# Block ends and routes of a graph convolution placed between node tiles of the next block, with what its scatters read kept for the program

## The chip, the cores and the metric

The kernel runs on one core of a Trainium2 chip, in one launch. The metric is the device time in microseconds (us) of one execution. A run of several executions gives a median; one execution is also recorded by the hardware profiler, and its span (first to last instruction) is what the views of the profile show. In these views PE is the matrix engine (TensorE), PEld its weight loads, DVE is VectorE, ACT is ScalarE, POOL is GpSimd and SP is SyncE. "L1431" is line 1431 of the kernel's source.

## The reference

The input is a matrix `x` of 3125 nodes by 256 features and 50,000 edges (`src`, `dst`). Four blocks follow each other, each on a normalised copy of `x` and each added to it:

```python
x = x + gcn(layernorm(x))       # three graph convolutions
x = x + ffn0(layernorm(x))      # 16 experts, 2 of them for each node
x = x + gat(layernorm(x))       # attention over the edges, 4 heads of 64
x = x + ffn1(layernorm(x))      # 8 experts, 2 of them for each node

# one graph convolution, three times (the third without relu)
h   = (h * norm_src[:, None]) @ W
agg = segment_sum(h[src], dst)
h   = relu(agg * norm_dst[:, None] + b)

# ffn0; ffn1 is of the same kind, with gelu
logits = x @ gate_w + gate_b
vals, idx = top_k(logits, 2);  w = softmax(vals)
y = x + sum_k w[k] * (relu(x @ w1[idx[k]] + b1[idx[k]]) @ w2[idx[k]] + b2[idx[k]])
y = layernorm(y) * gamma + beta
```

## The kernel before

**Nodes and stages.** The 3125 nodes lie in 25 node tiles (`NT`) of 125 real rows in 128 partitions. `X` holds the features, `HB` a normalised copy. The stages of the profiled execution are, in us of the span: the edges are counted into a dense matrix of counts in DRAM, `cnt`, and its transpose `cntT` (to about 308); the three convolutions (308 to 476, 476 to 641, 641 to 857); the plan of the first experts and the first experts (to about 1235); the attention, GAT (to about 1770); the second experts (to the end).

**A convolution.** The columns of `cnt` (destination nodes) are cut into seven blocks, `BLK`: four of 512 and three of 384 columns. At the start of a layer every node tile of `HB` is split into two parts, a rounded one and the rest, in `parts` (DVE L1417 and its neighbour, ACT L1419). Then, for each block, the 25 node tiles are taken in five groups of five. For a group the counts are loaded (`cload`, five DMAs a block on SP's queue) and cast on ACT to `ar` (L1426; two buffers). For each node tile four matrix products add to the two PSUM tiles `agg` (L1431), so a block has 100 of them. At the block's end `agg` is copied to `aT`, half by DVE (L1434) and half by ACT (L1435). For each of the block's three or four node tiles, PE multiplies `aT` by the layer's weights into `gout` (L1440), DVE scales it and adds the bias (`gy`, L1443), and ACT writes relu of it to `HB` (L1446); in the third layer (layer 2) DVE adds it to `X` (L1448) instead.

**A route.** After a block of layer 2, its rows are normalised again and routed: `moments` (DVE L692, L693, L695; the square root on ACT, L675; `newton` on DVE, L680 to L685), `normalise` (DVE, L703), and `R0.route`, which runs the generator `Router.steps` to its end. These steps are, in order:
- PE transposes the rows (L805) and ACT copies them to `hb` (L807), tile by tile; PE computes the gate's logits (L812).
- DVE finds the two best experts of each node (`lg`, L821, to L851). The rows are sent to DRAM (`keep`, POOL's queue, L785).
- A small tile `meta` of 8 values per node is filled: the node's number (L858), the second expert (L859), the two weights (the exponential on ACT, L866; L868 to L870), zeros (L871) and the number as an integer (L872). The combining weights `cw` follow (L876 to L878).
- `both` and `seen` count the nodes of each expert (L882 to L885), and two products on PE, L889 and L890, give `pr`, the place of each node within its expert. From it DVE computes `at`, with `off` for the padding rows (L899), and the places `at_i` (L903).
- POOL scatters one row block of `meta` after the other into `slots` in DRAM by these places (L905), eight for a block of four tiles. The scatters are declared independent of each other.

`meta`, `off` and `at_i` are taken from a pool with two buffers for each name, so a third route writes to the buffers of the first one.

After the last block `R0.plan` counts the tiles of each expert (L923 to L957). `experts` then reads the slots (`slot`, DMAs on ACT's queue, L1015), gathers rows (`xs`, POOL, L1017), transposes them (L1026), multiplies by the first weights (L1038; `w1t` loaded at L1003) and the second (L1048). At its beginning the combining weights are transposed and copied to `cT` (ACT, L1090), for the product with the second biases (L1099).

**The attention** runs over the same seven blocks on `cntT`. Its work at a block's end is already a generator, `finish`, of which one step is taken after each node tile of the next block; for every second block, and after the last, the last steps include `R1.steps`, the route of the second experts. All products on PE stand in one chain:

```python
if last:
    tc.add_manual_dep(m.ins, last[0].ins.name, ...)   # no semaphore: an order only
last[:] = [m]
```

**What sets the order.** Each engine executes its own list of instructions in order. A scheduler at build time makes these lists from the dependencies, the buffers' reuse and the order of the program's text, so an instruction can stand on its engine before or after others than the text shows. In the convolutions of the kernel before, no order is written out; in the attention the chain fixes PE's.

Of the kernel before, what the change touches and what calls it, by code (L numbers as in the profile page):

```python
# [19 lines left out]
P = 128  # L20
# [574 lines left out]
def fast(  # L595
# [68 lines left out]
    ns = consts.tile([P, NT], F32, name="ns")  # L664
# [70 lines left out]
    tok_i = consts.tile([P, NT], I32, name="tok_i")  # L735
    nc.gpsimd.iota(tok_i, pattern=[[P, NT]], base=0, channel_multiplier=1)

    class Router:


# [2 lines left out]
        def __init__(self, name, gate_w, gate_b, E, softmax, pool):  # L743
            self.name, self.E, self.softmax = name, E, softmax
            self.Q = E * NT + 3
            self.TT = -(-2 * N // P) + E
            self.slots = dram.tile([self.Q * P, 8], F32, name=f"slots_{name}")
            self.feats = dram.tile([NP, D], F32, name=f"feats_{name}")
            self.res = dram.tile([2 * NP + self.TT * P, D], F32, name=f"res_{name}")
            self.sent = []  # L750
            self.gwt = pool.tile([P, DC, E], F32, name=f"gw_{name}")
            nc.sync.dma_start(self.gwt, gate_w.rearrange("(c p) e -> p c e", p=P))
            self.gbt = row_bcast(gate_b, E, f"gb_{name}", pool)
            self.cw = pool.tile([P, NT, E], F32, name=f"cw_{name}")
# [32 lines left out]
        def steps(self, H, t0, U, work, psum, h0=None, pe=lambda i: i, kept=None):  # L787
# [4 lines left out]
            def wt(name, shape, dt=F32):  # L792
                return work.tile(shape, dt, name=f"{name}_{nm}", tag=f"{name}_{nm}")
# [58 lines left out]
                                                   op0=OP.mult, op1=OP.add)  # L852
                    cur = rest
            yield
            meta = wt("meta", [P, U, 8])
            if not kept:
                self.keep(H[:, h0:h0 + U, :], t0, U)
            nc.vector.tensor_copy(meta[:, :, 0], tok2[:, t0:t0 + U])  # L858
            nc.vector.tensor_scalar(meta[:, :, 1], firsts[1], float(E), None, op0=OP.add)  # L859
            if self.softmax:  # L860
                nc.vector.tensor_copy(meta[:, :, 2], tops[0])
# [1 line left out]
            else:  # L863
# [4 lines left out]
                nc.vector.tensor_scalar(p1, ex, 1.0, None, op0=OP.add)  # L868
                nc.vector.reciprocal(meta[:, :, 2], p1)
                nc.vector.tensor_mul(meta[:, :, 3], ex, meta[:, :, 2])  # L870
            nc.vector.memset(meta[:, :, 4:], 0.0)  # L871
            nc.vector.tensor_copy(meta.bitcast(I32)[:, :, 5], tok_i[:, t0:t0 + U])  # L872
            yield
            cw = self.cw[:, t0:t0 + U, :]
            w2 = wt("w2", [P, U, E])
            nc.vector.tensor_tensor(cw, hots[0], bc(meta[:, :, 2]), op=OP.mult)  # L876
            nc.vector.tensor_tensor(w2, hots[1], bc(meta[:, :, 3]), op=OP.mult)
            nc.vector.tensor_tensor(cw, cw, w2, op=OP.add)  # L878
            yield

            both = wt("both", [P, U, E], BF16)
# [12 lines left out]
            for i in range(2):  # L894
                at = wt(f"at{i}", [P, U])
                nc.vector.tensor_tensor(hots[i], hots[i], row, op=OP.mult)
                nc.vector.tensor_reduce(at, hots[i], axis=AX.X, op=OP.add)
                off = wt(f"off{i}", [P, U])
                nc.vector.tensor_scalar(off, drop[:, t0:t0 + U], float((E * NT + 1) * P + i * PADS), unreal,  # L899
                                        op0=OP.add, op1=OP.mult)  # L900
                nc.vector.scalar_tensor_tensor(at, at, real, off, op0=OP.mult, op1=OP.add)
                at_i = wt(f"at_i{i}", [P, U], I32)
                nc.vector.tensor_copy(at_i, at)  # L903
                for u in range(U):
                    d = nc.gpsimd.indirect_dma_start(  # L905
                        out=self.slots, out_offset=bass.IndirectOffsetOnAxis(ap=at_i[:, u:u + 1], axis=0),
                        in_=meta[:, u, :], in_offset=None)
# [492 lines left out]
    with tc.tile_pool(name="gcn", bufs=2) as gp, \  # L1400
            tc.tile_pool(name="gparts", bufs=1) as gh, \
            tc.tile_pool(name="gloads", bufs=3) as loads, \
            tc.tile_pool(name="ps_agg", bufs=2, space=PSUM) as ps_agg, \
            tc.tile_pool(name="ps_gout", bufs=2, space=PSUM) as ps_gout, \
            tc.tile_pool(name="ps_gmisc", bufs=2, space=PSUM) as ps_gmisc:
        def misc(shape):
            return ps_gmisc.tile(shape, F32, name="misc", tag="misc")

        R0.ready(f0_b1, f0_b2, plans)
        parts = gh.tile([P, NT, 2, D], F32R, name="parts")  # L1410
        for layer in range(3):
            for t in range(NT):
                if layer == 0:
                    nc.vector.tensor_scalar(HBn[:, t, :], X[:, t, :], mv[:, t, 0:1], rn[:, t:t + 1],
                                            op0=OP.subtract, op1=OP.mult)
                hi = gp.tile([P, D], F32, name="hi", bufs=3)
                nc.vector.tensor_single_scalar(hi.bitcast(I32), HBn[:, t, :D].bitcast(I32), -4096,  # L1417
                                               op=OP.bitwise_and)
                nc.scalar.copy(parts[:, t, 0, :], hi)  # L1419
                nc.vector.tensor_tensor(parts[:, t, 1, :], HBn[:, t, :D], hi, op=OP.subtract)  # L1420
            for b, (s0, w) in enumerate(BLK):
                agg = [ps_agg.tile([P, 512], F32, name=f"agg{f}") for f in range(DC)]
                for kg in range(0, NT, KG):
                    a = load_cnt(loads, cnt[b], kg, w)
                    ar = gp.tile([P, KG, 512], F32R, name="ar")
                    nc.scalar.copy(ar[:, :, :w], a[:, :, :w])  # L1426
                    for k in range(KG):
                        t = kg + k
                        for f in range(DC):
                            for i in range(2):  # L1430
                                nc.tensor.matmul(agg[f][:, :w], parts[:, t, i, f * P:(f + 1) * P], ar[:, k, :w],  # L1431
                                                 start=(t == 0 and i == 0), stop=(t == NT - 1 and i == 1))
                aT = gp.tile([P, DC, 512], F32, name="aT")
                nc.vector.tensor_copy(aT[:, 0, :w], agg[0][:, :w])  # L1434
                nc.scalar.copy(aT[:, 1, :w], agg[1][:, :w])  # L1435
                for u in range(w // P):
                    t = s0 // P + u
                    po = ps_gout.tile([P, D], F32, name="gout")
                    for f in range(DC):
                        nc.tensor.matmul(po, aT[:, f, u * P:(u + 1) * P], gw[layer][:, f, :],  # L1440
                                         start=(f == 0), stop=(f == DC - 1))
                    y = gp.tile([P, D], F32, name="gy", bufs=3)
                    nc.vector.scalar_tensor_tensor(y, po, nd[:, t:t + 1], gb[layer],  # L1443
                                                   op0=OP.mult, op1=OP.add)
                    if layer < 2:
                        nc.scalar.activation(HBn[:, t, :D], y, AF.Relu, scale=ns[:, t:t + 1])  # L1446
                    else:
                        nc.vector.tensor_add(X[:, t, :], X[:, t, :], y)  # L1448
                if layer == 2:
                    mv, r = moments(X, s0 // P, w // P)  # L1450
                    normalise(HBn, X, mv, r, s0 // P, w // P)
                    R0.route(HBn, s0 // P, w // P, gp, misc)
        R0.plan(plans, misc)

    gconst.__exit__(None, None, None)
# [26 lines left out]
    with tc.tile_pool(name="moe0", bufs=1) as mp:  # L1482
# [16 lines left out]
        with tc.tile_pool(name="ps_pre", bufs=2, space=PSUM) as ps, tc.tile_pool(name="tail", bufs=1) as mp:  # L1499
# [274 lines left out]
```

## Time and profile before

| what | value |
|---|---|
| median of 3 runs | 2113.64 us (2106.36 to 2114.82) |
| profiled execution's own time | 2094.98 us |
| its span | 2093.2 us, so 1.8 us lie around it |
| mean granted clock of PE | 0.956 |
| PE / DVE / ACT / POOL busy | 90% / 57% / 38% / 18% |
| sums of the convolutions, PE L1431 | 447.8 us in 2100 products |
| block-end products, PE L1440 | 78.3 us in 300, 20.5 us idle ahead of them |
| scatters of the routes, POOL L905 | 107.8 us in 100 |
| casts of the counts, ACT L1426 | 220.8 us in 105 |

Busy time is the sum of an engine's instructions; the idle time beside a group is what the engine stood still just before it, with the instruction or transfer whose end released it. In a timeline a row starts with the start in us and the time that the row covers, then engine, line, operation, tiles written and read, shapes and the number of instructions taken together; a bracket at the end is the idle time before it. In a chain of waits, the three numbers are us in total, number of waits and the longest. In the table of stretches the columns are the stretch, its length, then for PE, PEld, DVE, ACT and POOL the busy time with the number of instructions, then PE's granted clock (1.00 is full speed), the DMA share and GB/s. The profiled execution is 18.7 us shorter than the median of the runs.

### The profile page before, as it was taken

The page shows a single profiled execution, that of the slowest core. Times are in us where ns is not written, and L with a number is a line of the kernel's source. Part 1 is how long each engine was busy: PE and PEld are TensorE (multiplying, and loading weights), DVE is VectorE, ACT ScalarE, POOL GpSimd, SP SyncE. Part 2 cuts the span into 40 slices and gives each one's busy share as a digit, 9 for nine tenths or more (in the row PEclk, how much of TensorE's full clock was granted, in tenths as well). Part 3 has the DMA queues.
Part 4 walks back from the last instruction along what each step waited for, and adds up shares of the span by engine and source line. Part 5 has one row for each costly group of instructions (what it writes and reads, how often), then busy time and mean ns, then how long its engine had stood idle before and what let it go on. Part 6 is the DMA issues. An engine that isn't in the chain of part 4 may idle for free. (4 is left out here: it accounts for less than half of the span.)

```text
span 2093.2 us, 31963 instructions
## 1 busy us (share of the span) xinstructions
PE 1893.4 (90%) x10944; PEld 1252.0 (60%) x10944; DVE 1188.1 (57%) x3825; ACT 791.7 (38%) x1611; POOL 369.1 (18%) x414
## 2 busy tenths in 40 slices
PE   1898979999999898699998988999999998699997
PEld 1444548898898677588887741222223232588886
DVE  7998863131124344443332768899998998434330
ACT  0367766565555534222222561212212222222221
POOL 4000000000000312254443000000300402344430
PEclk9999989999999999789999989999999999599998
DMA  5145664344344333665664601111011110465656
GB/s 148 53 176 217 227 220 133 110 129 129 116 115 147 112 91 94 198 201 168 182 192 139 213 1 51 39 48 61 28 54 43 43 39 28 122 182 164 193 160 197
DMA packets 172299, 259.91 MB, mean 124 GB/s; under 512 B 33476, under 2 KB 116658, under 8 KB 171100
## 3 DMA queue, kind: packets, MB, share of 16 engines
q1 hardware_dynamic: 148446, 211.87, 32.6%
q0 software_dynamic: 16016, 37.00, 5.6%
q10 hardware_dynamic: 7662, 8.84, 1.3%
q8 instruction: 93, 1.52, 0.3%
q14 instruction: 82, 0.67, 0.1%
HBM read 187.38 MB, written 70.27 MB: 123 GB/s over the span
## 5 line engine op out<-in xcount | busy, mean ns | idle before, releaser
L1431 PE MATMUL agg<-ar,parts 128*128 128x512 f32 (+1 forms) x2100 | 447.8, 371 | 7.6 <-ACT parts L1419 7.6
L1431 PEld LDWEIGHTS agg<-ar,parts 128*128 128x128 f32 x2100 | 383.6, 189 | 55.0 <-ACT parts L1419 7.7
L1702 DVE SCALAR_TENSOR_TENSOR HB<-ub,wj,cload 128x512 f32<-128x512 f32 (+1 forms) x420 | 268.6, 689 | 21.2 <-ACT ub L1606 9.9
L1426 ACT CAST ar<-cload 128x2560 fp32r<-128x2560 f16 (+1 forms) x105 | 220.8, 2103 | 147.1 <-PE agg L1431 133.5
L1038 PE MATMUL ph<-xsT,w1t 128*128 128x128 f32 x1792 | 239.2, 285 | 12.2 <-DVE xsT L1028 11.1
L1042 ACT ACTIVATE hid<-ph,b1s 128x128 f32<-128x128 f32 x448 | 128.1, 369 | 322.0 <-PE ph L1038 310.1
L1038 PEld LDWEIGHTS ph<-xsT,w1t 128*128 128x128 f32 x1792 | 220.4, 196 | 47.0 <-DVE xsT L1028 30.5
L1048 PE MATMUL py<-w2all,hid 128*128 x896 | 211.9, 380 | 0.0
L1590 PE MATMUL att<-HB,xp 128*64 128x512 f32 (+1 forms) x840 | 187.5, 567 | 0.0
L1048 PEld LDWEIGHTS py<-w2all,hid 128*128 128x128 f32 x896 | 162.1, 191 | 17.5
L1326 DVE TENSOR_SCALAR od<-ramp,by 128x450 f16<-128x450 f16 (+11 forms) x588 | 152.3, 320 | 22.1 <-PE pc L1328 21.0
L1434 DVE COPY aT<-agg 128x512 f32<-128x512 f32 (+1 forms) x21 | 13.3, 633 | 248.5 <-PE agg L1431 248.5
L1328 PE MATMUL pc<-od,os 128*128 128x450 f16 (+11 forms) x588 | 136.6, 334 | 17.6 <-DVE od L1326 9.5
L1059 DVE TENSOR_TENSOR to_i<-to,two 128x1 int32<-128x1 f32 x112 | 17.7, 158 | 237.4 <-DMA res_m<-y,to_i 237.4
L1065 POOL DMA_INDIRECT res_m<-y,to_i x112 | 110.4, 986 | 232.6 <-DVE y L1064 228.3
L905 POOL DMA_INDIRECT slots_m<-meta_m,at_i_m x100 | 107.8, 1078 | 209.0 <-DVE at_i_m L903 122.2
L1331 ACT CAST cr<-pc 128x400 f16<-128x400 f32 (+10 forms) x202 | 95.5, 503 | 63.8 <-PE pc L1328 48.9
L1017 POOL DMA_INDIRECT xs<-feats_m,slot x112 | 108.3, 967 | 61.7 <-issue 23.8
L1590 PEld LDWEIGHTS att<-HB,xp 128*64 128x64 f32 x840 | 51.8, 137 | 107.7 <-issue 61.1
L1328 PEld LDWEIGHTS <-os 128*128 128x128 f16 x588 | 62.2, 118 | 77.9 <-DVE od L1326 20.6
L1590 PE MATMUL sums<-HB,pj 128*32 128x512 f32 (+1 forms) x840 | 102.6, 561 | 0.0
L1440 PE MATMUL gout<-g0w,aT 128*128 128x256 f32 x300 | 78.3, 417 | 20.5 <-DVE aT L1434 15.7
(332 smaller groups left out, 2350.0 us busy)
## 6 DMA issues: line engine op xcount, KB each, us to landing
cload<-cnt SPq DMA_DIRECT2D x60, 640.0 KB
w1t<-in_L_ffn_w_dram SPq DMA_DIRECT2D x56, 512.0 KB
w1t<-in_L_ffn_W_dram SPq DMA_DIRECT2D x52, 512.0 KB
cload<-cnt SPq DMA_DIRECT2D x45, 480.0 KB
cntT<-ct SPq DMA_DIRECT2D x100, 128.0 KB
cnt<-cr SPq DMA_DIRECT2D x4, 3200.0 KB
cload<-cntT SPq DMA_DIRECT2D x20, 640.0 KB
r<-res_m SPq DMA_DIRECT2D x50, 256.0 KB
```

Source lines behind the costliest of these rows:

```text
L905: d = nc.gpsimd.indirect_dma_start(out=self.slots, out_offset=bass.IndirectOffsetOnAxis(ap=at_i[:, u:u + 1], axis=0), in_=meta[:, u, :], i ...
L1017: nc.gpsimd.indirect_dma_start(out=xs, out_offset=None, in_=self.feats, in_offset=bass.IndirectOffsetOnAxis(ap=slot[:, 5:6].bitcast(I32), ...
L1038: behind(nc.tensor.matmul(ph[:, c, :], w1t[:, f, c * P:(c + 1) * P], xsT[:, f, :], start=(f == 0), stop=(f == DC - 1)), "PE")
L1042: nc.scalar.activation(hid[:, c, :], ph[:, c, :], func, bias=self.b1s[:, c, j:j + 1])
L1048: behind(nc.tensor.matmul(py, hid[:, c, :], w2all[:, bass.ds(r, 1), c, :].rearrange("p o d -> p (o d)"), start=(c == 0), stop=(c == FC - 1 ...
L1065: d = nc.gpsimd.indirect_dma_start(out=self.res, out_offset=bass.IndirectOffsetOnAxis(ap=to_i, axis=0), in_=y, in_offset=None)
L1326: nc.vector.tensor_scalar(od[:, :w * NT], ramp[:, :w * NT], by[1][:, j:j + 1], None, op0=OP.is_equal)
L1328: nc.tensor.matmul(pc[:, :w * NT], os_[:, :, j % OS], od[:, :w * NT], start=(k == 0), stop=(k == c - 1))
L1426: nc.scalar.copy(ar[:, :, :w], a[:, :, :w])
L1431: nc.tensor.matmul(agg[f][:, :w], parts[:, t, i, f * P:(f + 1) * P], ar[:, k, :w], start=(t == 0 and i == 0), stop=(t == NT - 1 and i == 1))
L1590: return chain(nc.tensor.matmul(*args, **kw))
L1702: nc.vector.scalar_tensor_tensor(e[:, h, :w], ub[:, h, :w], wj[:, t, h:h + 1], a[:, k, :w], op0=OP.max, op1=OP.mult)
```

## The change

Four things are changed.

1. All products of the convolutions on PE stand in one chain. The work at a block's end is a generator, `finish`, with the copies to `aT` first; then after each node tile of the next block one step is taken: the products of one node tile in a step, then (in layer 2) an empty step, `moments`, `normalise`, an empty step, and the steps of the route. In layers 0 and 1 the last node tiles (22 to 24) are split into `parts` within the last block's `finish`, and the next layer begins with the first 22. After the last block all steps are run to the end before the plan.
2. `metas` (8 values for all 25 tiles), `places` and, in each router, `off` are tiles kept for the program, filled at its start as far as they don't depend on the data. A route writes its own slice of them.
3. `Router.steps` has one more empty step ahead of `both`; the attention runs the same steps, so its count products (L889, L890) come one node tile later in PE's chain.
4. `lr`, a small tile of the attention, is taken from another pool.

```diff
+    metas = consts.tile([P, NT, 8], F32, name="metas")
+    nc.vector.memset(metas, 0.0)
+    nc.vector.tensor_copy(metas[:, :, 0], tok2)
+    nc.vector.tensor_copy(metas.bitcast(I32)[:, :, 5], tok_i)
+    places = consts.tile([P, 2, NT], I32, name="places")
...
+            self.off = pool.tile([P, 2, NT], F32, name=f"off_{name}")
+            for i in range(2):
+                nc.vector.tensor_scalar(self.off[:, i, :], drop, float((E * NT + 1) * P + i * PADS), unreal,
+                                        op0=OP.add, op1=OP.mult)
...
-            meta = wt("meta", [P, U, 8])
+            meta = metas[:, t0:t0 + U, :]
             if not kept:
                 self.keep(H[:, h0:h0 + U, :], t0, U)
-            nc.vector.tensor_copy(meta[:, :, 0], tok2[:, t0:t0 + U])
...
-            nc.vector.memset(meta[:, :, 4:], 0.0)
-            nc.vector.tensor_copy(meta.bitcast(I32)[:, :, 5], tok_i[:, t0:t0 + U])
             yield
             cw = self.cw[:, t0:t0 + U, :]
...
+            yield
             yield
 
             both = wt("both", [P, U, E], BF16)
...
-                off = wt(f"off{i}", [P, U])
-                nc.vector.tensor_scalar(off, drop[:, t0:t0 + U], float((E * NT + 1) * P + i * PADS), unreal,
-                                        op0=OP.add, op1=OP.mult)
+                off = self.off[:, i, t0:t0 + U]
                 nc.vector.scalar_tensor_tensor(at, at, real, off, op0=OP.mult, op1=OP.add)
-                at_i = wt(f"at_i{i}", [P, U], I32)
+                at_i = places[:, i, t0:t0 + U]
...
+        def finish(layer, b, agg):
+            s0, w = BLK[b]
+            aT = gp.tile([P, DC, 512], F32, name="aT")
+            nc.vector.tensor_copy(aT[:, 0, :w], agg[0][:, :w])
+            nc.scalar.copy(aT[:, 1, :w], agg[1][:, :w])
+            yield
+            for u in range(w // P):
+                t = s0 // P + u
+                po = ps_gout.tile([P, D], F32, name="gout")
+                for f in range(DC):
+                    chain(nc.tensor.matmul(po, aT[:, f, u * P:(u + 1) * P], gw[layer][:, f, :],
+                                           start=(f == 0), stop=(f == DC - 1)))
+                y = gp.tile([P, D], F32, name="gy", bufs=3)
+                nc.vector.scalar_tensor_tensor(y, po, nd[:, t:t + 1], gb[layer], op0=OP.mult, op1=OP.add)
+                if layer < 2:
+                    nc.scalar.activation(HBn[:, t, :D], y, AF.Relu, scale=ns[:, t:t + 1])
+                    if b == len(BLK) - 1:
+                        split(t)
+                else:
+                    nc.vector.tensor_add(X[:, t, :], X[:, t, :], y)
+                yield
+            if layer == 2:
+                yield
+                mv, r = moments(X, s0 // P, w // P)
+                yield
+                normalise(HBn, X, mv, r, s0 // P, w // P)
+                yield
+                yield
+                yield from R0.steps(HBn, s0 // P, w // P, gp, misc, pe=chain)
+
+        ends = []
+
+        def step():
+            while ends and next(ends[0], ends) is ends:
+                ends.pop(0)
...
-            for t in range(NT):
+            late = BLK[-1][0] // P if layer else NT
+            for t in range(late):
...
-                                nc.tensor.matmul(agg[f][:, :w], parts[:, t, i, f * P:(f + 1) * P], ar[:, k, :w],
-                                                 start=(t == 0 and i == 0), stop=(t == NT - 1 and i == 1))
+                                chain(nc.tensor.matmul(agg[f][:, :w], parts[:, t, i, f * P:(f + 1) * P], ar[:, k, :w],
+                                                       start=(t == 0 and i == 0), stop=(t == NT - 1 and i == 1)))
+                        step()
+                if layer < 2:
+                    while ends:
+                        step()
+                end = finish(layer, b, agg)
+                next(end)
+                ends.append(end)
+        while ends:
+            step()
         R0.plan(plans, misc)
...
-    lr = g1.tile([P, NT, 2, NH], F32, name="lr")
...
+            lr = mp.tile([P, NT, 2, NH], F32, name="lr")
```

`chain` is the function quoted above, now also for the convolutions; `split` holds the three operations that fill `parts`.

More of the change, by code (lines that the diff above doesn't have):

```diff
@@ L1410, in fast, with chain, split @@
         parts = gh.tile([P, NT, 2, D], F32R, name="parts")
+        last = []
+        def chain(m):
+            if last:
+                tc.add_manual_dep(m.ins, last[0].ins.name, mybir.DependencyInfo(
+                    mybir.DependencyClass.NoSync, mybir.DependencyReason.DATA), reason="in this order")
+            last[:] = [m]
+            return m
+        def split(t):
+            hi = gp.tile([P, D], F32, name="hi", bufs=3)
+            nc.vector.tensor_single_scalar(hi.bitcast(I32), HBn[:, t, :D].bitcast(I32), -4096,
+                                           op=OP.bitwise_and)
+            nc.scalar.copy(parts[:, t, 0, :], hi)
+            nc.vector.tensor_tensor(parts[:, t, 1, :], HBn[:, t, :D], hi, op=OP.subtract)
@@ L1415, in fast @@
                                             op0=OP.subtract, op1=OP.mult)
[L1416 to L1420, printed above, removed]
+                split(t)
             for b, (s0, w) in enumerate(BLK):
@@ L1430, in fast @@
                             for i in range(2):
-                                nc.tensor.matmul(agg[f][:, :w], parts[:, t, i, f * P:(f + 1) * P], ar[:, k, :w],
-                                                 start=(t == 0 and i == 0), stop=(t == NT - 1 and i == 1))
[L1433 to L1452, printed above, removed]
+                                chain(nc.tensor.matmul(agg[f][:, :w], parts[:, t, i, f * P:(f + 1) * P], ar[:, k, :w],
[9 more added lines that the diff above has]
+            step()
         R0.plan(plans, misc)
```

## The prediction

> **What bounds the kernel now.** I read the page first: the engines' totals and the 40 slices.
>
> ```profile
> span 2093.2 us, 31963 instructions
> PE 1893.4 (90%) x10944; PEld 1252.0 (60%) x10944; DVE 1188.1 (57%) x3825; ACT 791.7 (38%) x1611; POOL 369.1 (18%) x414
> PE   1898979999999898699998988999999998699997
> PEclk9999989999999999789999989999999999599998
> ```
>
> PE is busy 90% of the span, so only PE's gaps and the slices with a lowered clock can give time back. A slice is 52.3 us. Among the weak ones are the 14th, the 16th and the 17th (680 to 733 and 785 to 890 us): the third convolution (layer 2), then the plan. So next come PE's and DVE's chains of waits there (PE over 640:900, DVE over 641:860).
>
> ```profile
> PE gout L1440 <- DVE aT L1434: 15.7, 5, 4.5
> PE gout L1440 <- DVE gy L1443: 4.8, 1, 4.8
> ```
>
> ```profile
> DVE meta_m L858 <- DMA slots_m<-meta_m,at_i_m: 48.1, 5, 11.8
> ```
>
> PE waits 20.5 us ahead of block-end products, for the copy `aT`. DVE itself waits 48.1 us to overwrite `meta`, until the route before has scattered it. The timelines join the two:
>
> ```profile
> 697.78 0.17 DVE L858 COPY meta_m<-tok 128x4 f32<-128x4 f32 x1 [11.80 <-DMA slots_m<-meta_m,at_i_m]
> ...
> 698.08 0.68 DVE L1434 COPY aT<-agg 128x512 f32<-128x512 f32 x1
> ```
>
> ```profile
> 682.07 12.28 PE L1431 MATMUL agg<-ar,parts 128*128 128x512 f32 x53
> 698.82 5.12 PE L1440 MATMUL gout<-g0w,aT 128*128 128x256 f32 x16 [4.47 <-DVE aT L1434]
> ```
>
> PE ends the sums at 694.35, DVE stands at the meta copy until 697.78, `aT` is behind it in DVE's order, and PE starts at 698.82. The same 16 products take 3.72 us in layer 1 (at 498.92), here 5.12. The stretches by block show why:
>
> ```profile
> 641.00:668.00 27.00, 27.00 (x121) 22.19 (x121) 5.76 (x17) 14.67 (x13) 0.00 (x0) 1.00 0.41 124
> 704.00:740.00 36.00, 32.26 (x143) 25.63 (x141) 15.93 (x72) 16.31 (x14) 8.57 (x9) 0.91 0.35 107
> ```
>
> The first block has no such wait and a granted clock of 1.00; a block with the wait takes 9 us more and has 0.91.
>
> **Part 1, layer 2: the old cost.** Layer 1 (475.99 to 641.28) does the same sums and products without idling: 26.3 us per 512 block, 20.0 per 384 block, 165.2 in all. Layer 2 goes from 641.28 to the last sum at 854.5: 213.2 us. It does the same, less the last block's products (3 x 0.84 = 2.5), plus PE's share of six routes (3.55 us for four 512 blocks, 2.7 for two 384 ones, from the rows of transposes, logits and counts: 19.6). Undisturbed that is 165.2 - 2.5 + 19.6 = 182.3. So 30.9 us are there: 20.5 of waits and 10.4 of lowered clock. The kept tiles take away what DVE waited for: each route writes its own slice of `metas` and `places`. The fixed chain puts sums of the next block between the products.
>
> **The new wait.** The built program's order on ScalarE shows what is late next. Before, the Sqrt of a route stood ahead of the third cast `ar` of the next block. Now it stands behind it, and that cast cannot start before the block's fifth node tile is summed, since two buffers hold `ar`. The durations:
>
> ```profile
> L1426 ACT CAST ar<-cload 128x2560 fp32r<-128x2560 f16 x19 | 44.3, 2332 | 32.5 <-PE agg L1431 24.9 <-issue 7.6
> L1426 ACT CAST ar<-cload 128x1920 fp32r<-128x1920 f16 x15 | 27.0, 1798 | 16.3 <-PE agg L1431 14.2 <-ACT ex_m L866 2.1
> L675 ACT ACT_TABLE_LOAD x6 | 7.7, 1283 | 0.1
> ```
>
> From the start of a 512 block: a node tile's sums are 4 x 0.2307 = 0.92 us, a product pair 0.84; five tiles with four pairs end at 7.98; the cast 2.33, the table 1.28; from Sqrt to the first transpose 1.80 (859.78 to 861.58 in the last route): 13.4. PE reaches the transposes after tile 8, at 11.7, and waits 1.75; in the block without the table load 0.45. The same working gives 2.1 where a 512 block is routed under a 384 one and 2.8 twice after 384 blocks: 0.45 + 2 x 1.75 + 2.1 + 2 x 2.8 = 11.6 us. The copies `hb` fall behind the fourth cast in the same queue: about 0.45 four times at a transpose and 1.25 twice at the logits, 4.3. Together 15.9 us, queued behind it in the fixed chain all further sums.
>
> **The clock behind such waits.** In the GAT stage PE has two waits of this size:
>
> ```profile
> 1635.40 0.19 PE L890 MATMUL misc<-seen_m,ones 128*128 128x64 bf16 x1 [1.77 <-DVE seen_m L885]
> 1635.52 0.91 PE L1590 MATMUL pl<-xT,wlb 64*128 64x384 f32 x2
> 1636.36 2.28 PE L1590 MATMUL att<-e,xp 128*64 128x384 f32 x8
> 1638.57 1.51 PE L1590 MATMUL sums<-e,pj 128*32 128x384 f32 x8
> ```
>
> Behind 1.77 us of waiting, eight `att` take 2.28 (1.51 in the next undisturbed group), eight `sums` 1.51 (0.85): 1.4 lost; behind 1.74 at 1759.59 it is 1.6. A wait of 0.85 (at 1486) lost nothing. At 1.6 for four of the five waits of about 1.75 or more (the fifth partly overlaps the low clock of another), 6.4. Layer 2: -30.9 + 15.9 + 6.4 = -8.6, taken as -9. Bounds: no new wait at all -31; twice the new waits and their clock loss +14, less if the waits overlap, for which I use -2 as the near bound and leave the rest to the third rival.
> The Trainium skill, "TensorE: Matmul & The Clock Gate", section "Why this matters for your kernels", says that only idle gaps of more than about 3 us between bursts throw the clock back. By that rule the 6.4 would fall away and layer 2 would come out near -15; the rows at 1635 and 1759 speak against it here.
>
> **Part 2, GAT: one empty step more.** It moves the count products (L889, L890) one node tile later, while DVE's `seen` keeps its place. PE's waits for `seen` are 4.5 us (4 of them), and the low clock behind two is 3.0: at most -7.5. The extra tile covers each wait only in part where the chain needed more. DVE is nearly as busy as PE there, so some comes back: -4.5 (-1 to -7.5).
>
> **Part 3, from route to experts.** The tile `cT` lay in memory that `meta` had used:
>
> ```profile
> 882.71 1.05 ACT L1090 COPY cT<-misc 16x512 f32<-16x512 f32 x2 [14.66 <-DMA slots_m<-meta_m,at_i_m]
> 883.44 1.32 ACTq L1003 DMA_DIRECT2D w1t<-in_L_ffn_w_dram  x2
> 885.28 4.57 ACTq L1015 DMA_DIRECT2D slot<-slots_m  x6
> ```
>
> All scatters have landed at 882.7; only then come `cT`, two weight loads, and at 885.28 the slots that the first gather needs. With `meta` kept elsewhere, `cT` and the loads go ahead during the wait, and the slots follow the scatters directly: -2.5. At the second start the rows read the same (1800.56, slots at 1802.92): -2.5. Sum -5 (-2 if the slots' landing is not what starts the experts, -7 with the clock).
>
> **Part 4, the start, and small edits.** Nine small operations fill `metas` and `off` (about 0.7 us of DVE, ahead of `edge`). In the built order POOL now clears `HB` (about 2.8 us) before the first gather `got` (33.21), and DVE makes its `acc` operations ahead of the one-hots, where it stood 2.3 us idle at 44 and 3.95 us in one L774 operation (0.34 its like) beside POOL's memset. That clear must wait for transfers that landed somewhere between 22 and 34.3; if by 30.4 it delays nothing. Estimate -3 (-5 to +4). Copies and memsets dropped from the first GAT route and the GCN's prologue: -0.6. The second empty place, `lr` in another pool, has no row: 0. In layers 0 and 1 the products are only spread between sums; eight transposes spread between sums at 780.89 to 782.33 cost 0.13 each, nothing extra: 0.
>
> **Sum.** -9 - 4.5 - 5 - 3 - 0.6 = -22.1 us. The profiled execution took 2094.98 (span 2093.2, 1.8 outside), so about 2073 of its kind. It is 18.7 under the median of 2113.64; I carry the microseconds to the median: 2091.5, so 2091.
>
> **The rivals.**
> *First, the waits cost no clock, or hardly arise* (a table load earlier, a shorter Sqrt chain). For: PE kept a clock of 1.00 through a wait of 0.85. Against: the two GAT rows. Without clock loss layer 2 gives -15, the total -28, 2085; without any wait -31 and -44, 2069. Chance 0.18.
> *Second, layer 2's gain is eaten*: the copy on ScalarE of the second half of `aT`, the casts and `hb` queue up so that PE waits 31 us again, or DVE still waits for scatters because the kept tile is followed as a whole (then the change doesn't do what it says; its slices are distinct and the built order lists no such wait). Only parts 2 to 4 remain: -13, 2100.5. Chance 0.14.
> *Third, slower*: Sqrt comes to lie behind the fourth cast too. Then the first transpose waits 2.33 + about 2 more, 4.1; `hb` and logits 2.5 each; and the low clock lasts over 6 us of work, 3 lost: 12 per block, 72 for six. 72 - 31 - 13 = +28, 2141. It turns slower than before at (31 + 13) / 6 = 7.3 us per block. For: ScalarE executes in order and is the only place that Sqrt can go; against: the built order has Sqrt directly behind the third cast. Chance 0.06.
> *Fourth, the start*: POOL's clear holds the first gather back until its transfers land, +8 in place of -3: 2102. Chance 0.05.
> The forecast keeps 0.57.
>
> **How the numbers follow.** Half a per cent, 10.6 us, is about what a measurement of this kernel can tell from no change: faster means under 2103.1, slower over 2124.2. Faster: 0.53 of the forecast's 0.57, all of the first rival, 0.08 of the second, 0.02 of the fourth: 0.81. Same: 0.04 + 0.06 + 0.03 = 0.13. Slower: 0.06. Range: low 2069, the first rival's end; high 2108, where parts 2 to 4 sit at -1, -2 and +0 and layer 2 at -2 to -3. Outside are the third rival and the tails of the others.
>
> **What would show it.** Right: no DVE wait for `slots_m`; no PE idle ahead of `gout`; layer 2 near 204 us; new PE waits of 1.7 to 2.8 us for `HB` (L703) at the transposes, each followed by a clock near 0.5; none for `seen` in GAT; `cT` not released by a scatter; the first expert transposes 2.5 us sooner behind the plan. Wrong: PE waits of 4 us at transposes, or a clock of 1.00 behind waits of 2 us, or the first sum of layer 0 later than 308.

## The result, and the profile after

The changed kernel takes 2084.38 us (median of 4 runs, 2082.53 to 2092.98) beside 2110.0 us of the kernel before (4 runs, 2104.91 to 2114.82): a ratio of 0.9887, 95% interval 0.9847 to 0.9927. A second comparison (6 runs against 11) gave 0.991, 0.9879 to 0.994. The forecast was 2091.0, or 22 us less; the two ratios are 24 and 19 us less. It is faster by more than half a per cent in both, over the whole of both intervals.

The page of the profiled execution (2083.14 us) begins:

```profile
span 2081.3 us, 31883 instructions
PE 1890.9 (91%) x10944; PEld 1257.5 (60%) x10944; DVE 1196.2 (57%) x3777; ACT 791.2 (38%) x1611; POOL 365.3 (18%) x414
PE   1898979999999988699997979999999998799997
PEclk9999989999999999699999979999999999699998
```

PE has the same instructions, DVE 48 fewer. The chain of waits of PE over 630:900 has lost its first line of before:

```profile
PE misc L816 <- DVE HB L703: 18.8, 7, 4.2
...
PE misc L823 <- ACT hb_m L818: 1.0, 2, 0.5
...
PE misc L816 <- ACT hb_m L818: 0.4, 1, 0.4
PE gout L1446 <- DVE aT L1439: 0.3, 1, 0.3
```

The wait ahead of `gout` has gone from 15.7 us to 0.3. In its place PE waits 18.8 us for `HB` ahead of the route's first transposes; 4.15 of these are in the last route, which nothing covered before either, and 14.7 are new. On DVE (637:860) no wait for a scatter is left; the longest waits are now:

```profile
DVE lg_m L832 <- PE misc L823: 34.0, 7, 6.1
DVE aT L1439 <- PE agg L1489: 33.0, 7, 17.6
DVE rs_r L680 <- ACT rs_s L675: 13.3, 7, 3.0
```

The third line, DVE waiting for the Sqrt on ACT (1.6 us before), names the new wait's source. One block in the timelines of PE and of ACT:

```profile
698.34 4.93 PE L1489 MATMUL agg<-ar,parts 128*128 128x512 f32 x20
705.62 0.41 PE L816 MATMUL misc<-ident,HB 128*128 128x128 f32 x2 [2.35 <-DVE HB L703]
705.79 1.93 PE L1489 MATMUL agg<-ar,parts 128*128 128x512 f32 x4
```

```profile
700.17 2.34 ACT L1484 CAST ar<-cload 128x2560 fp32r<-128x2560 f16 x1 [5.77 <-issue]
702.52 1.28 ACT L675 ACT_TABLE_LOAD   x1
703.82 0.21 ACT L675 ACTIVATE rs_s<-ve 128x4 f32<-128x4 f32 x1
```

The cast and the table stand ahead of the Sqrt, PE stands from 703.27 to 705.62, and the four sums behind the wait take 1.93 us instead of 1.17: the clock is low.

The stage marks of all profiled executions, in us. A length runs from the start of the first product named to the end of the last. "Layer 2" runs from its first sum to its last (before: 638.3 to 854.3; the prediction counted from 641.28, behind the products of layer 1, so its 204 is about 207 here).

| kernel | first sum of layer 0 | layer 2 | last sum to first expert product | products of the first experts | products of the attention | last of these to the second experts' first | span |
|---|---|---|---|---|---|---|---|
| before | 308.4 | 216.0 | 39.6 | 244.9 | 529.0 | 42.2 | 2093.2 |
| before, again | 307.4 | 216.8 | 39.6 | 250.1 | 531.4 | 42.5 | 2107.2 |
| changed | 304.4 | 207.9 | 37.8 | 241.0 | 529.7 | 39.6 | 2081.3 |
| changed, again | 304.9 | 204.3 | 37.7 | 250.2 | 533.3 | 39.6 | 2088.3 |
| kept_only | 305.3 | 188.5 | 36.9 | 243.1 | 532.3 | 39.4 | 2059.6 |
| kept_yield | 304.8 | 189.1 | 37.3 | 252.1 | 531.7 | 40.0 | 2070.8 |
| steps_only | 308.4 | 224.1 | 39.7 | 254.4 | 528.7 | 42.2 | 2116.6 |
| later_one | 304.2 | 203.9 | 37.5 | 241.0 | 533.2 | 39.5 | 2078.0 |
| later_three | 304.3 | 188.2 | 37.9 | 247.2 | 528.5 | 41.0 | 2064.9 |
| sqrt_first | 305.1 | 191.5 | 37.7 | 245.2 | 533.2 | 39.4 | 2070.5 |

### The profile page after: what moved, and what is told of

Read it like the earlier page. It is cut to its first block, busy times and chain, and to the rows that moved or that the text cites. A ratio compares the mean times of both kernels' runs of the same rounds, so it can differ in the third digit from the quotient of the medians.

```text
span 2081.3 us, 31883 instructions
## 1 busy us (share of the span) xinstructions
PE 1890.9 (91%) x10944; PEld 1257.5 (60%) x10944; DVE 1196.2 (57%) x3777; ACT 791.2 (38%) x1611; POOL 365.3 (18%) x414
## 4 chain that ended last, share of the span: by engine, by line
PE 65%; issue 10%; DVE 9%; ACT 5%; DMA 5%; POOL 4%; another core or an unknown queue 0%; POOLq 0%; SPq 0%; ACTq 0%; DVEq 0%
PE agg L1489 19%; PE att L1637 14%; PE sums L1637 7%; PE ph L1045 4%; PE py L1055 3%; DMA res_m<-y,to_i 3%; DVE od L1333 2%; PE gout L1446 2%; POOL xs L1024 2%; PE pc L1335 2%; PE misc L1157 2%; PE rsum L1157 2%; POOL res_m L1072 2%; PE pt L1344 2%; PE pl L1637 1%
## 5 line engine op out<-in xcount | busy, mean ns | idle before, releaser
L1489 PE MATMUL agg<-ar,parts 128*128 128x512 f32 (+1 forms) x2100 | 473.8, 380 | 7.6 <-ACT parts L1432 7.6
L1489 PEld LDWEIGHTS agg<-ar,parts 128*128 128x128 f32 x2100 | 388.4, 192 | 56.2 <-ACT parts L1432 7.7
L1749 DVE SCALAR_TENSOR_TENSOR HB<-ub,wj,cload 128x512 f32<-128x512 f32 (+1 forms) x420 | 268.4, 684 | 20.7 <-ACT ub L1653 10.9
L1049 ACT ACTIVATE hid<-ph,b1s 128x128 f32<-128x128 f32 x448 | 127.7, 368 | 323.1 <-PE ph L1045 252.1
L912 POOL DMA_INDIRECT slots_m<-metas,places x100 | 103.2, 1032 | 231.9 <-DVE places L910 182.7
L1749 DVE SCALAR_TENSOR_TENSOR spare<-ub,wj,cload 128x512 f32<-128x512 f32 (+1 forms) x140 | 89.8, 684 | 7.5 <-PE sums L1637 4.1
```

The source lines that it names most:

```text
L912: d = nc.gpsimd.indirect_dma_start(out=self.slots, out_offset=bass.IndirectOffsetOnAxis(ap=at_i[:, u:u + 1], axis=0), in_=meta[:, u, :], i ...
L1049: nc.scalar.activation(hid[:, c, :], ph[:, c, :], func, bias=self.b1s[:, c, j:j + 1])
L1489: chain(nc.tensor.matmul(agg[f][:, :w], parts[:, t, i, f * P:(f + 1) * P], ar[:, k, :w], start=(t == 0 and i == 0), stop=(t == NT - 1 and ...
L1749: nc.vector.scalar_tensor_tensor(e[:, h, :w], ub[:, h, :w], wj[:, t, h:h + 1], a[:, k, :w], op0=OP.max, op1=OP.mult)
```

## The experiments

**before_again: how far does one profile carry?** No edit.

> The kernel before, unchanged. Its shown profile took 2094.98 us and its timed runs 2104.91 to 2114.82, while the changed kernel's profile and runs agree (2083.14, against 2082.53 to 2092.98). Theory: the kernel before has a stage whose length differs between executions by 10 to 20 us, and a second profile shows in which; if this profile again takes about 2095, the profiled executions are simply shorter for this kernel. Stage marks of the first profile to compare: first sum of layer 0 at 308.43, layer 2 from 641.28 to 854.5, first expert transpose at 892.43, first attention product at 1241.3, last at 1764.6, span 2093.2. Rival: each of the stages varies a little, by 1 to 3 us, as the clock's low spells fall.

Timed 0.9995 of before (0.9978 to 1.0013). This profile's span is 2107.2, 14.0 more than the first one's. The difference is not in one stage: 5.2 in the products of the first experts, 1.9 between these and the attention, 2.4 in the attention, 3.0 in the second experts, under 1 elsewhere. So both readings hold a part: the experts vary most. What the change moves (the first, second, third and sixth columns) repeats within 1 us. The profile in which the forecast was worked out was a short execution, and the pair of first profiles shows only 11.9 us of the timed difference.

**kept_only: the kept tiles without chain and steps.** Of the diff, only `metas`, `places` and `off` with what fills them at the start (and `lr`, to make room):

```diff
+    metas = consts.tile([P, NT, 8], F32, name="metas")
...
+    places = consts.tile([P, 2, NT], I32, name="places")
...
-            meta = wt("meta", [P, U, 8])
+            meta = metas[:, t0:t0 + U, :]
...
-                at_i = wt(f"at_i{i}", [P, U], I32)
+                at_i = places[:, i, t0:t0 + U]
```

> The kernel before with only the tiles kept for the program (metas, places, off), and lr in the other pool. PE's order in the convolutions is that of before to the instruction. Theory: DVE's wait for the scatters was all that held layer 2; without it aT is copied at once, the transposes stand as far behind the products as before, where they waited for nothing, and Sqrt stands ahead of the third cast. Layer 2 then takes 183 to 187 us (213.2 before, 204.9 in the changed kernel), with no low clock in it: about 18 to 20 us less than the changed kernel, so about 2065. First sum of layer 0 at 304.4 as in the changed kernel, since the start has the same instructions. Rival: without the chain the products at the block ends wait for something else (aT behind the casts on ACT), and layer 2 takes 200 us or more.

2069.75 us, ratio 0.9823 (0.9786 to 0.986). Layer 2 takes 188.5 us; the theory said 183 to 187 in the other count, 186 to 190 in this one. The theory stands, its rival has fallen. PE's waits there (630:830), and the table of stretches over layer 2 of this kernel and of the changed one:

```profile
PE gout L1444 <- DVE gy L1447: 0.9, 3, 0.3
PE misc L814 <- DVE HB L703: 0.5, 1, 0.5
PE gout L1444 <- issue: 0.3, 1, 0.3
```

```profile
636.00:824.50 188.50, 186.40 (x945) 157.94 (x943) 91.21 (x393) 100.12 (x92) 45.87 (x49) 1.00 0.39 115
```

```profile
634.00:842.00 208.00, 191.83 (x945) 166.97 (x944) 97.98 (x393) 100.77 (x93) 44.99 (x47) 0.95 0.35 104
```

With PE's old order and free tiles, PE's waits come to 1.7 us and the clock is 1.00 throughout. In layer 2 the chain and the steps cost the changed kernel 16 to 19 us of what the kept tiles gain.

**steps_only: the chain and the steps with the old `meta`, `at_i` and `off`.**

```diff
-            meta = metas[:, t0:t0 + U, :]
+            meta = wt("meta", [P, U, 8])
...
-                at_i = places[:, i, t0:t0 + U]
+                at_i = wt(f"at_i{i}", [P, U], I32)
```

> The changed kernel with meta, off and at_i taken from the two-buffer pool again, so only the chain, the steps and the empty step are changed against before. Theory: the meta copy stands in DVE's order behind the first product's addition of the next block, so the copy aT is no longer held, but the following gy are, for as long as the scatters two routes back last; those started some 10 us earlier than the meta copy, so DVE waits 0 to 8 us there; then Sqrt, already late, comes later by that. Layer 2 between 205 and 230 us. First sum of layer 0 at 308.4, as before. Rival: the steps alone remove the wait, since PE's products are spread; layer 2 as in the changed kernel, 205.

2115.62 us, ratio 1.0024 (1.0006 to 1.0041): alone, chain and steps gain nothing. Layer 2 takes 224.1 us, 8 more than before. The first sum stands at 308.4, so the gain at the start belongs to the kept tiles. DVE waits for the scatters again, and PE behind it, now in the middle of the products:

```profile
DVE meta_m L860 <- DMA slots_m<-meta_m,at_i_m: 31.1, 5, 7.1
```

```profile
703.56 1.28 PE L1442 MATMUL gout<-g0w,aT 128*128 128x256 f32 x4 [4.28 <-DVE gy L1445]
...
712.08 0.41 PE L807 MATMUL misc<-ident,HB 128*128 128x128 f32 x2 [1.24 <-DVE HB L703]
```

**sqrt_first: the changed kernel with the Sqrt ahead of the third cast.** PE's order is the same to the instruction.

```diff
+                    m = nc.scalar.copy(ar[:, :, :w], a[:, :, :w])
+                    if layer == 2 and b > 0 and kg == 2 * KG:
+                        tc.add_manual_dep(m.ins, roots[0].ins.name, ...)   # roots: the last Sqrt
```

> The changed kernel with one order more on ACT: in layer 2 the Sqrt of a route stands ahead of the third cast of the block, as it did before the change. PE's chain is the same to the instruction. Theory: that order alone made PE wait for HB at the first transposes (0.37, 2.35, 2.36, 3.80, 2.91, 2.91 us) and brought the low clock. Sqrt can then run at about 8.5 us of a block and HB is ready at about 11, ahead of PE's 11.7; the waits at the first transposes are under 0.5 us, there is no low clock from 670 to 840, and layer 2 takes 186 to 191 us in place of 207.9, so the kernel 16 to 22 us less than the changed one. Rival: the third cast, now behind the Sqrt and its table load, comes too late for its sums, and PE waits there instead by about as much.

2079.27 us, ratio 0.9839 (0.981 to 0.9869); layer 2 191.5 us (207.9 and 204.3 in the changed kernel; 186 to 191 expected), with a mean clock of 0.99 in it: one low stretch of 3.4 us was left, behind the logits and not behind a wait for `HB`. The waits for `HB` at first transposes shrink from 14.7 us in six to 3.8 in three, of which one is long, in the block where a 512 block is routed under a 384 one:

```profile
733.43 0.41 PE L818 MATMUL misc<-ident,HB 128*128 128x128 f32 x2 [0.58 <-DVE HB L705]
...
764.05 0.41 PE L818 MATMUL misc<-ident,HB 128*128 128x128 f32 x2 [2.54 <-DVE HB L705]
...
810.89 0.41 PE L818 MATMUL misc<-ident,HB 128*128 128x128 f32 x2 [0.71 <-DVE HB L705]
```

So the order of one instruction on ACT accounts for 12.8 to 16.4 of the 15.8 to 19.4 us that the chain and the steps cost in layer 2. No wait of PE for a cast took its place.

**later_three: the changed kernel with three more empty steps ahead of the route.**

```diff
                 normalise(HBn, X, mv, r, s0 // P, w // P)
                 yield
                 yield
+                yield
+                yield
+                yield
```

> The changed kernel with three more empty steps between normalise and the route, so that PE meets the first transpose after node tile 11 in place of 8: 2.77 us later under a 512 block, 2.12 under a 384 one. Theory: its waits there were 0.37, 2.35, 2.36, 3.80, 2.91 and 2.91 us; what stays is at most 0.8 to 1.7 in three blocks, under the size behind which the clock fell. Layer 2 takes 184 to 190 us, and the kernel 14 to 20 us less than the changed one. Rival: Sqrt and the copies hb move back in ACT's order as well, and the waits stay at about 2 us; no gain.

2066.77 us, ratio 0.9791 (0.9752 to 0.983); layer 2 188.2 us, clock 1.00. Most of the same waits are taken away from the other side: PE comes later rather than Sqrt earlier. One wait of 1.98 us is longer than the 1.7 expected, and the clock stayed at 1.00 behind it too.

```profile
PE misc L816 <- DVE HB L703: 3.4, 3, 2.0
PE misc L823 <- ACT hb_m L818: 1.0, 3, 0.3
PE misc L816 <- ACT hb_m L818: 0.7, 1, 0.7
```

**later_one: one empty step more.**

> The changed kernel with one more empty step, not three, between normalise and the route: PE meets the transposes one node tile later (0.92 us under a 512 block, 0.71 under a 384 one). On ACT the first copy hb falls behind the fourth cast with it. Theory: the waits at the first transposes shrink by just that, to 0, 1.4, 1.4, 2.5 to 3, 2.2 and 2.2 us, with some 0.5 more at the third one for hb, and the clock falls only behind those of which more than about 1.6 us lie in one of the stretches of 3.41 us in which the profile's clock changes: not in the second and third route, perhaps in the last three. Layer 2's sums take 196 to 203 us. Rival: any wait above 1 us lowers the clock, and layer 2 takes 204 or more.

One execution: layer 2 takes 203.9 us, above the theory's 196 to 203 and just under the rival's 204. The waits for `HB` were 2.16, 2.14, 3.83, 5.08 and 2.21 us, hardly shorter: the third cast itself began 9.31 us behind ACT's `aT` (689.48 to 698.79), against 8.58 in the changed kernel (691.59 to 700.17), so `HB` moved back with PE. The delay does not begin on ACT. DVE's `gy`, which needs only the fourth product pair (ended on PE at 696.59 here, at 698.69 in the changed kernel), begins at 698.69 and 700.07, each time 0.1 us ahead of the cast, and the profile names PE as what released it. So both seem to have waited for a signal of PE that came late. Why it came late, and later here, is not settled, and the question of the wait that lowers the clock is not answered by this run as it was meant to be.

**kept_yield: kept_only with the empty step, for the attention.**

```diff
             nc.vector.tensor_tensor(cw, cw, w2, op=OP.add)
             yield
+            yield
```

> The kept tiles alone (as kept_only) with the one empty step more in the route, which reaches only the attention, since the convolutions run the route to its end at once. Theory: PE's waits for seen at the count products (0.84, 1.76 and 1.74 us in kept_only) vanish, but DVE's products for the sums of the same blocks become what PE waits for, in small bits, since DVE is busy 95% of the time there: the blocks in which the count products lie shorten by 1 to 3.5 us, the following ones lengthen by 1 to 3, and from the first block's end to the last it takes 434 to 435 us against 438.2 in kept_only, at most 4 us less. Rival (the prediction's term): the waits and their low clock come off in full, 7 us less, 431. Either way the best version so far with later_three, at about 0.980 of before.

2073.53 us, ratio 0.9805 (0.9777 to 0.9833), not to be told from kept_only. PE's three waits for `seen`, 4.3 us in kept_only, are gone. But block by block (from the transposes at the ends of the attention's blocks) the second to the seventh take 79.3, 83.2, 82.0, 66.4, 65.0 and 61.5 us where kept_only has 79.3, 84.2, 81.4, 69.9, 62.9 and 60.4: 437.5 against 438.2. The block with the longest wait gains 3.5, and the two behind it give 3.2 back. That is less than the theory's 3 to 4 and far from the 7 of the prediction's upper end.

**after_again: the changed kernel with more rounds.**

> The changed kernel, unchanged, once more beside the next three and with more rounds. Theory: the stage lengths that the change moves repeat within 1 us (first sum of layer 0 at 304.4, layer 2's sums 207.9 us, from the last sum to the first expert product 37.8, from the last attention sum to the second experts' first product 39.6), while the experts' stage, 244.9 and 250.1 us in two profiles of before and 241.0 in the changed kernel's, moves by several us by itself. These stages sum to -16 to -17 us against before; the timed ratio then comes out between 0.989 and 0.993. Rival: the experts' stage is shortened by the change as well, by some 6 us; then it lies at 241 to 243 again and the ratio near 0.989.

2093.39 us, ratio 0.991 (0.9879 to 0.994). The start, and both ways from a route to its experts, repeat within 0.5 us; layer 2 does not, 204.3 against 207.9, and the first experts take 250.2 us, where the rival wanted 241 to 243. Their stage moves by itself: 241.0 to 254.4 over ten profiles, 241.0 and 250.2 for this one kernel.

## Why the prediction was right, and where not

**Layer 2, -9: right in sum, and the terms nearly so.** Measured -8.1 and -11.7 against the first profile of before (216.0 to 207.9 and 204.3). The new wait was named with its place and cause, and sqrt_first shows that cause. Its size: 0.37, 2.35, 2.36, 3.80, 2.91 and 2.91 us, 14.7 together, where the working had 0.45, 1.75, 1.75, 2.1 and twice 2.8, 11.6. The step that was short is the start of the third cast: it was put at the end of the fifth node tile's sums (699.27 in the block shown), and ACT begins it at 700.17. The waits for `hb` were put at 4.3 and came to 1.4. Together 16.1 against 15.9: two errors that cancel, which is luck. The low clock was put at 6.4 us. The trace has 20.5 us at half clock in layer 2, at most 10.2 lost, and the second profile 10.2 us, at most 5.1 lost. PE's busy time in layer 2, 191.8 and 187.7 us, is 8.9 and 4.8 us above the 182.9 of later_three, which does the same products at full clock. So the term has no fixed size; 6.4 lies inside. With the old cost of -30.9 these terms make -5.9 and -9.5 (the second profile's waits are 16.6 us); about 2 us of the gain are in none of them.

Two of the prediction's own signs came out against it. It asked for a clock near 0.5 behind each new wait and named a clock of 1.00 behind waits of 2 us as a sign of being wrong: the clock stayed at 1.00 behind the wait of 2.91 us that ends at 799.66, and in the second profile behind one of 2.44 and one of 2.91. And one wait came near the 4 us that it named: 3.80, and 3.94 in the second profile.

**The clock rule.** The clock was low behind the wait of 2.35 us and behind one of the two of 2.91 us, as behind two in the attention of before; behind the other of 2.91 us it was not. The first rival, built on no loss, was not what happened. The Trainium skill, "TensorE: Matmul & The Clock Gate", section "Why this matters for your kernels", has about 3 us as the gap to avoid. The traces of this case have low clock behind 1.77 us, so the measurement decides.

**The start, -3: right, and by its mechanism.** 308.4 and 307.4 became 304.4 and 304.9. Before:

```profile
33.21 1.13 POOL L1276 DMA_INDIRECT got<-eds,at_e  x1 [15.03 <-DVE at_e L1274]
...
56.42 0.97 POOL L1276 DMA_INDIRECT got<-eds,at_e  x1 [15.68 <-DVE od L1326]
```

In the changed kernel POOL's clear did wait for transfers, until 31.93, and the first gather came 1.7 us later:

```profile
31.93 2.79 POOL L781 MEMSET HB<- 128x3224 f32 x1 [13.88 <-DMA res_m<-HB]
34.89 1.13 POOL L1283 DMA_INDIRECT got<-eds,at_e  x1 [0.17 <-issue]
...
52.58 0.97 POOL L1283 DMA_INDIRECT got<-eds,at_e  x1 [12.47 <-DVE od L1333]
```

Most of the 1.7 us is not the clear's: DVE makes the addresses `at_e` at 34.25 in place of 32.76, 1.5 us later; the operations that fill the kept tiles stand ahead of them and were put at 0.7 us. The second gather, which DVE's `acc` operations hold back, came at 52.58 in place of 56.42, and the end of the stage goes with it: in the ten profiles it stands at 52.6 to 53.4 with the first sum at 304.2 to 305.3, or at 56.4 with the first sum at 307.4 to 308.4. steps_only, with the old start, has the old 308.4. One reading of the working was off: the 0.34 us that it set beside the 3.95 us of a L774 operation are those of one of half the width (203 columns in place of 403); the same operation of full width takes 2.06 us in the changed kernel.

**From route to experts, -5: right.** 39.6 to 37.8, and 42.2 to 39.6: -1.8 and -2.6, where the working had -2.5 twice. `cT` no longer waits for a scatter:

```profile
865.06 0.57 ACT L1097 COPY cT<-misc 16x512 f32<-16x512 f32 x1 [9.12 <-issue]
...
871.38 4.57 ACTq L1022 DMA_DIRECT2D slot<-slots_m  x6
```

**The attention, -4.5: wrong.** The waits for `seen` went as forecast; the time did not come off: 529.0 and 531.4 us before, 529.7 and 533.3 in the changed kernel. The step that failed is the value taken between -1 and -7.5: DVE makes what the products take (`e` and its ring, L1749) and is nearly as busy as PE: in the fifth block 62.28 of 69.9 us before and 59.25 of 66.4 after, in the sixth 58.48 of 62.1 and 60.53 of 64.9. PE, no longer held by the count products, caught up with it. In the sixth block a row of eight products `att` took 1.51 us before:

```profile
1657.30 1.51 PE L1590 MATMUL att<-HB,xp 128*64 128x384 f32 x8
```

In the changed kernel such rows stretch. The second fence has what DVE makes for the first of the two rows:

```profile
1642.81 3.19 PE L1637 MATMUL att<-HB,xp 128*64 128x384 f32 x8 [0.17 <-DVE HB L1749]
...
1646.71 2.47 PE L1637 MATMUL att<-e,xp 128*64 128x384 f32 x8
```

```profile
1642.14 0.61 DVE L1749 SCALAR_TENSOR_TENSOR HB<-ub,wj,cload 128x384 f32<-128x384 f32 x1
...
1643.01 0.61 DVE L1749 SCALAR_TENSOR_TENSOR HB<-ub,wj,cload 128x384 f32<-128x384 f32 x1
...
1643.88 0.62 DVE L1749 SCALAR_TENSOR_TENSOR HB<-ub,wj,cload 128x384 f32<-128x384 f32 x1
...
1644.51 0.58 DVE L1749 SCALAR_TENSOR_TENSOR HB<-ub,wj,cload 128x384 f32<-128x384 f32 x1
```

The granted clock is 1.00 there. Four such operations feed a row of eight, and the fourth ends at 1645.09, while the row runs from 1642.81 to 1646.00. The chain of waits shows 0.2 us of it, because the recorded times of the products overlap and cover the gaps between their starts. The working should have taken the bound from DVE's own work in the block, not from PE's waits. That DVE sets the pace is read from these rows and from kept_yield, where the blocks behind give back what one gains; no run gives DVE less to do there. The low clock, priced at 3.0 us behind two waits, was no fixed cost either: in the second profile of before it falls behind one of them alone.

**The total.** The four stages that moved sum to -3.3 (start), -10.3 (layer 2), -1.8 and -2.8, 18.2 us, from the means of two profiles each. The forecast's 22.1 is 4 more, which is mostly the attention's term; the 0.6 for dropped small operations no column shows by itself. The timed ratios, 24 and 19 us less, lie on both sides of it; what they hold beyond the 18.2, 1 to 6 us, is inside their intervals and within what the experts' stage does by itself. Whether the change moves that stage is open. The spans of the same profiles differ by 15.4 us on average, since other stages went the other way. One of these repeats: from PE's last product to the end of the span it is 6.1 to 6.4 us in the three profiles without the kept tiles and 7.6 to 8.2 in the seven with them, about 1.5 us that no term has; its cause is open. Layers 0 and 1 together took 329.9 us before and 329.6 in the changed kernel, so their 0 was right. The rival that made the kernel slower needed the Sqrt behind the fourth cast; it stood behind the third.

## What to carry to other kernels

Ask of each part of a change what it is worth alone: here the kept tiles gave the gain (0.9823), the chain and steps gave nothing by themselves (1.0024) and took 16 to 19 us of it away in layer 2, until one instruction's place on ACT, or three empty steps, brought the kernel level with the kept tiles alone (0.9839 and 0.9791, in place of 0.9887 and 0.991). When PE's order is fixed by hand, work out for each product in it when its operand can be there, with what stands ahead on the engine that makes it. A wait on a busy engine may be worth little if a second engine is nearly as busy in the same block: price it by that engine's work.

## What the runs showed of the hardware

In the ten traces the granted clock changes only at whole steps of 3.41 us: in layer 2 of the changed kernel its low spells start at 678.62, 705.93, 740.06, 770.78 and 825.39, which lie 8, 10, 9 and 16 steps apart. Whether a wait cost clock goes, in the rows below, with how it lay across the steps. In the table of stretches of the changed kernel, cut at these steps:

```profile
794.68:798.09 3.41, 2.07 (x12) 1.75 (x11) 0.39 (x3) 3.29 (x3) 1.94 (x2) 1.00 0.13 18
798.09:801.50 3.41, 1.84 (x12) 1.84 (x13) 2.89 (x11) 0.74 (x2) 0.79 (x1) 1.00 0.43 130
801.50:804.90 3.40, 2.91 (x23) 2.78 (x22) 0.31 (x2) 3.10 (x3) 0.00 (x0) 1.00 0.39 123
821.98:825.39 3.41, 0.68 (x4) 0.35 (x3) 1.21 (x7) 1.96 (x3) 0.00 (x0) 1.00 0.01 2
825.39:828.80 3.41, 3.24 (x12) 3.17 (x13) 1.68 (x6) 0.75 (x2) 0.79 (x1) 0.50 0.32 113
```

Two waits of the same 2.91 us: the one to 799.66 is cut in two by a step, PE is busy 2.07 and 1.84 us of the two stretches, and the clock stays at 1.00; the one to 825.56 lies in one stretch, PE is busy 0.68 us of it, and the next stretch has 0.50. In the attention of before a stretch with 1.64 us busy was followed by 0.50 as well. So in these rows the clock fell behind a stretch with 1.64 us of 3.41 or less, and not behind one with 1.84 or more. That is no sharp border: in the second profile of the changed kernel the clock stayed at 1.00 behind stretches with 1.49 and 1.57 us busy.

```profile
702.41:705.82 3.41, 1.49 (x9) 1.30 (x10) 2.88 (x12) 0.75 (x4) 0.37 (x1) 1.00 0.47 174
705.82:709.24 3.42, 2.98 (x16) 2.16 (x15) 0.68 (x3) 3.17 (x4) 0.43 (x1) 1.00 0.59 168
821.87:825.28 3.41, 1.57 (x11) 1.57 (x12) 2.90 (x11) 0.81 (x4) 0.77 (x1) 1.00 0.01 2
825.28:828.70 3.42, 2.94 (x23) 2.81 (x22) 0.11 (x1) 3.03 (x4) 0.02 (x1) 1.00 0.33 115
```

One low stretch of the changed kernel, at 678.6, does not fit by busy time: PE is busy 2.97 us of the stretch before it, which holds the logits, 16 products of 16 columns, and a wait of 0.44 us. sqrt_first has one like it at 708.2, behind 2.98 us busy. What else counts is open.

In the two profiles of the changed kernel the steps lie within about 0.1 us of each other (one at 705.93, one at 705.82), but the waits do not: the one that ends at 705.62 in the first ends at 704.33 in the second. That they lie differently across the steps fits the 20.5 us at half clock in the one profile and the 10.2 in the other.
